# Turning the slot weights (and, in the second slot stage, the normalized tokens) by VectorE and through memory instead of by TensorE, in a three-stage layer on one core

## The chip, the cores and the metric

The kernel runs on one core of one Trainium2 chip. The metric is the device time of one execution in microseconds (us). A core has TensorE (PE in the profile, with its weight loads as PEld), VectorE (DVE), ScalarE (ACT), GpSimd (POOL), SyncE (SP, which here only issues DMAs), and 16 DMA engines between its on-chip memory SBUF and the chip's memory. TensorE's results go to PSUM, from which ACT or DVE copy them to SBUF.

## What is computed

The input x is 16 sequences of 512 tokens with 256 features, in 32-bit floats. The layer is

```
x = x + 0.5 * slot_ffn(layernorm(x))
x = x + attention(layernorm(x))      # causal, rotary, 16 heads of 64
x = x + 0.5 * slot_ffn(layernorm(x)) # the same weights as the first

def slot_ffn(x):
    q = broadcast(slot_query, (16, 16, 256))       # 16 slots for each sequence
    o = q + mha(q, x, x, d_*)                      # "dispatch": the slots gather from 512 tokens, 16 heads of 16
    h = layernorm(o) * ln_g + ln_b                 # slot e has its own expert e
    u, g = silu(h[e] @ W1[e] + b1[e]), silu(h[e] @ Wg[e] + bg[e])
    o = o + (u * g) @ W2[e] + b2[e]                # 16 experts, three weights of 1 MB each
    return mha(x, o, o, c_*)                       # "combine": the tokens read from 16 slots
```

## The kernel before

There are three stages in a row: slot FFN (n = 0), attention, slot FFN (n = 1). x stays in SBUF throughout. TensorE executes its instructions in program order. For ACT, DVE, POOL and SP a scheduler arranges the order in the slot FFN, while the attention is written under `manual_schedule`, in program order.

**Dispatch, the part that is changed.** A loop runs over the 16 sequences ("batches") i, with steps at different distances. The scores of the 256 pairs of slot and head (`FH * NS`, two halves c of 128) against 512 tokens come from one folded matrix `qk`, so each batch needs:

- `normalized` (L216): the layer norm h, with the tokens on the partitions, four DVE instructions. `pair_stats` and `pair_rstd` make mean and 1/std for two batches (PB) at a time.
- `width_first` (L223): hT, with the features on the partitions, by eight TensorE transposes of 128x128 into PSUM, one copy by ACT, one by DVE.
- `slot_weights` (L442): scores p_ds (L449, four matmuls that show as eight records), the row maximum by DVE (L451), its bias by POOL, exp by ACT (L454) into `at`, reciprocals by DVE, scaling by POOL (L458).
- `weights_transposed` (L461): `at` has the slots on the partitions; atT has the tokens there. Eight TensorE transposes p_atT (L467), one copy by ACT (L471), one by DVE (L473).
- `slot_sums` (L476): p_z (L480, 8 matmuls, 16 records), h against atT, copied by DVE into zT (L482).

TensorE's order in an iteration is hT(i), atT(i-2), ds(i-1), z(i-2). After every fourth batch `gathered` (L484) multiplies zT by the value weights (p_mo, 64 records). `half_of_slots` brings half of the slots through output projection (p_o) and layer norm to hE and hET.

**Weights.** `Experts.more` issues one expert weight of 1 MB (48 in all) on SP per call. The first 8 (EARLY) have buffers of their own and are loaded up front; four more (BUFS = 12) lie in pools that take over memory of the dispatch, and the rest follow as buffers come free. Loads 8 and later wait for the last p_mo of the dispatch, whose memory they take. The constants of the stage (`for_slots`, L245: sqbo, dbo, ln_g, ln_b, c_Wk, c_Wv, c_Wq, d_Wo, c_Wo, cbo) and in the first stage the rows of biases are issued on SP ahead of them. `queries(b)` (L366) makes combine's queries p_cq (L369) for batch b; they are spread as fillers through dispatch's end and the experts.

**Attention.** 64 units, a batch with four heads each, in a loop over u = -2 .. 63 in which the steps of units u to u+3 are mixed. For a unit, `exps` makes scores and weights pr, `normalize` scales them on POOL (L864), `Weights.turn` transposes blocks of 32x32 on DVE into sq (L879), `move` (L896) puts the blocks into their places with 16 DMAs of 160 KB on SP, sq to prT, and `sums` (L904, p_av L913) multiplies by the values v (`values`, L805). `leave` (L924) projects the result (p_ay, L929), adds it to x (DVE, L933) and, for a batch's last unit, writes x out (L935). At the end of the loop (u = 62, 63) no new units stand beside these steps.

The functions that the change touches:

Of the kernel before, what the change touches and what calls it, by code (L numbers as in the profile page):

```python
# [15 lines left out]
P = 128  # L16
# [15 lines left out]
EARLY, BUFS = 8, 12  # L32
# [15 lines left out]
def macaron_kernel(ctx: ExitStack, tc: tile.TileContext, a: dict, out: bass.AP):  # L48
# [19 lines left out]
    def by_width(t):  # L68
        return t.rearrange("p (c s) -> p c s", c=NC)

# [80 lines left out]
    def more_constants(su, later):  # L151
# [19 lines left out]
        def pieces():  # L171
# [5 lines left out]
            for k, br in enumerate(brs):  # L177
                for l in range(NL):
                    i = k * NL + l
                    nc.tensor.transpose(pt[:, i * n:(i + 1) * n], br.rearrange("r (p l) -> r l p", l=NL)[:, l],  # L180
                                        ident[:n, :n])
                    nc.vector.tensor_copy(b1g[:, k].rearrange("p e (l q) -> p l e q", l=NL)[:, l],
# [5 lines left out]
    mvs, rstds = {}, {}  # L188
# [18 lines left out]

    def pair_rstd(g, parts=1):
        rstds[g] = small.tile([P, PB * NT], F32, tag=f"rstd{g}", name=f"rstd{g}", bufs=1)
        n = PB * NT // parts  # L210
        for i in range(parts):
            inverse_std(rstds[g][:, i * n:(i + 1) * n], mvs[g][:, i * n:(i + 1) * n, 1], n, f"g{g}_{i}")

    def normalized(pool, b, bufs):

        h = pool.tile([P, NT, D], F32, tag="h", name=f"h{b}", bufs=bufs)  # L216
        for t in range(NT):
            i = (b % PB) * NT + t
            nc.vector.tensor_scalar(h[:, t, :], xs[b][:, t, :], mvs[b // PB][:, i, 0:1],
                                    rstds[b // PB][:, i:i + 1], ALU.subtract, ALU.mult)  # L220
        return h

    def width_first(h, b, hT, c):  # L223

        pt = ps(f"p_hT{b}_{c}")
        for t in range(NT):
            nc.tensor.transpose(pt[:, t * P:(t + 1) * P], h[:, t, c * P:(c + 1) * P], ident)
        if c == 0:
            nc.scalar.copy(hT[:, c, :], pt)
        else:  # L230
            nc.vector.tensor_copy(hT[:, c, :], pt)


    def ffn(n, last, ahead=None):
        with ExitStack() as es:
# [6 lines left out]
            with tc.tile_pool(name=f"early{n}", bufs=1) as ew, tc.tile_pool(name=f"slots{n}", bufs=1) as ss:  # L242
                w = {nm: ss.tile([P, NC, D], F32, tag=nm, name=nm) for nm in ("c_Wk", "c_Wv", "c_Wq")}
# [66 lines left out]
    def slots_and_experts(n, ss, load, w, for_slots, hTs, kT, vT):  # L310
# [52 lines left out]
        def queries(b):  # L363

            pqs = []
            for c in range(NC):  # L366
                pq = ps(f"p_cq{b}_{c}")
                for k in range(NC):
                    nc.tensor.matmul(pq, w["c_Wq"][:, k, c * P:(c + 1) * P], hTs[b][:, k, :],  # L369
                                     start=(k == 0), stop=(k == NC - 1))  # L370
                pqs.append(pq)
            qT = by_width(place(b, f"cq{n}_"))
            for c in range(NC):
                bias = bcol[:, R_CBQ + c:R_CBQ + c + 1]
                if c == 0:
                    nc.scalar.activation(qT[:, c, :], pqs[c], AF.Identity, bias=bias)
                else:
                    nc.vector.tensor_scalar(qT[:, c, :], pqs[c], bias, 1.0, ALU.add, ALU.mult)
            hTs[b] = qT

        with tc.tile_pool(name=f"disp{n}", bufs=2) as dp:
            hs, ats, zT = {}, {}, None
            constants = more_constants(dp, ss) if n == 0 else None
            tail = None
            load.more(EARLY)

            def norm(b):

                if b >= NB:
                    return  # L390
                if b % PB == 0 and (n == 0 or b >= 2 * PB):
                    pair_rstd(b // PB, PB if b == 0 else 1)
                hs[b] = normalized(dp, b, 4)
                if n == 0 and b % PB == 0 and b + PB < NB:
                    pair_stats(b // PB + 1)

            if n == 0:
                pair_stats(0)
            norm(0)
            norm(1)  # L400
            for i in range(NB + 2):
                if i < NB:
                    hTs[i] = by_width(place(i, f"hT{n}_"))
                    for c in range(NC):
                        width_first(hs[i], i, hTs[i], c)
                if i > 2:
                    atT = weights_transposed(dp, i - 2, ats.pop(i - 2))
                if 0 <= i - 1 < NB:
                    ats[i - 1] = slot_weights(dp, i - 1, hTs[i - 1])
                if i == 2:  # L410
                    atT = weights_transposed(dp, 0, ats.pop(0))
                if i == 5 and n == 0:
                    constants()
                if i > 0:
                    norm(i + 1)
                if i >= 2:
                    b = i - 2
                    if b % GB == 0:
                        if b > 0:
# [651 lines left out]
```

## Time and profile before

| | us |
|---|---|
| three timed runs | 2405.11, 2413.08, 2414.31 (median 2413.08) |
| the profiled execution | 2407.17, of which the span of its instructions is 2405.5 |
| dispatch, first stage: first p_ds to end of the last p_mo | 20.80 to 178.92 |
| first stage: experts from the first p_u to the last weights' landing | 191.44 to 288.70 |
| end of the attention's last p_ay | 1998.99 |
| dispatch, second stage: first p_ds to end of the last p_mo | 2006.86 to 2156.70 |
| second stage: the last weights' landing | 2266.21 |

Times in a profile are those of one execution, counted from the start of its span. A line of the timeline or of the chain of waits gives start, length, engine, source line, and how many records ("x8") it takes together; what ended an idle time before it stands behind it in brackets. An fp32 matmul shows as two records. Names such as p_ds or atT are the program's tiles with the numbers left out; L numbers are lines of the kernel before.

### The profile page before, as it was taken

How to read it: one execution, taken by the hardware profiler on the slowest of the kernel's cores; microseconds unless marked ns; L12 is line 12 of the kernel's file. 1: busy time of each engine (PE TensorE's matmuls, PEld its weight loads, DVE VectorE, ACT ScalarE, POOL GpSimd, SP SyncE). 2: the span in 40 equal slices, each digit the busy share in tenths (PEclk: the TensorE clock that was granted, in tenths of full speed). 3: DMA queues.
4: the chain of work that ended last, by engine and by line, in shares of the span. 5: the costliest groups of instructions: out<-in, count | busy, mean ns of one | idle time of the engine just before them, and what ended most of it. 6: DMA issues, size and time to landing. Idle time of an engine off the chain costs nothing.

```text
span 2405.5 us, 42349 instructions
## 1 busy us (share of the span) xinstructions
PE 2331.0 (97%) x14656; PEld 1463.5 (61%) x14656; DVE 1774.9 (74%) x4671; ACT 1069.5 (44%) x2919; POOL 1065.6 (44%) x1692
## 2 busy tenths in 40 slices
PE   7999989899999999999999999999999988999899
PEld 5765478456555555565655555656565555765488
DVE  8542288788888888988888888888888864542287
ACT  4333233355455555554545545545555443323233
POOL 2220044556565655565656555556465531210043
PEclk9999999999999999999999999999999998999999
DMA  9009951254545454545454545455555455019834
GB/s 316 13 2 374 360 126 62 47 120 107 122 107 127 102 132 102 124 108 122 107 131 98 133 105 118 111 118 111 123 107 128 109 130 188 1 44 377 315 110 136
DMA packets 142476, 323.16 MB, mean 134 GB/s; under 512 B 37236, under 2 KB 84408, under 8 KB 134072
## 3 DMA queue, kind: packets, MB, share of 16 engines
q1 hardware_dynamic: 141676, 319.93, 50.1%
q8 instruction: 116, 1.90, 0.3%
q14 instruction: 96, 0.79, 0.1%
q10 hardware_dynamic: 588, 0.54, 0.1%
HBM read 135.84 MB, written 16.78 MB: 63 GB/s over the span
## 4 chain that ended last, share of the span: by engine, by line
PE 83%; DVE 3%; DMA 2%; ACT 2%; SPq 1%; issue 1%; POOL 0%; DVEq 0%; ACTq 0%; POOLq 0%
PE p_as L844 12%; PE p_av L913 12%; PE p_v L805 9%; PE p_k L784 9%; PE p_ay L929 9%; PE p_q L784 9%; PE p_cy L661 4%; PE p_cq L369 4%; PE p_z L480 2%; PE p_ds L449 2%; PE p_cs L630 2%; PE p_u L522 2%; DMA w<-in_e_Wg_dram 1%; ACT pr L856 1%; PE p_catT L651 1%; PE p_y L549 1%
## 5 line engine op out<-in xcount | busy, mean ns | idle before, releaser
L864 POOL TENSOR_SCALAR pr<-pr,ars 128x512 f32<-128x512 f32 (+3 forms) x1024 | 523.6, 532 | 656.0 <-DVE ars L861 656.0
L856 ACT ACTIVATE pr<-pr,amn 128x512 f32<-128x512 f32 (+3 forms) x1024 | 561.6, 550 | 462.2 <-DVE amn L852 462.2
L852 DVE CUSTOM_DVE_ANT_0 pr<-p_as,causal 128x512 f32<-128x512 f32 (+3 forms) x1024 | 434.3, 484 | 98.5 <-PE p_as L844 97.0
L879 DVE STREAM_TRANSPOSE sq<-pr 128x768 f32<-128x768 f32 (+2 forms) x448 | 381.6, 907 | 17.4 <-issue 13.0
L844 PE MATMUL p_as<-k,q 32*128 32x512 f32 (+3 forms) x4096 | 332.1, 449 | 3.6 <-POOL k L795 3.6
L913 PE MATMUL p_av<-prT,v 128*64 128x512 f32 (+3 forms) x2048 | 296.0, 442 | 22.2 <-DMA c_Wk<-in_c_Wk_dram 9.1
L844 PEld LDWEIGHTS p_as<-k,q 32*128 32x128 f32 x4096 | 179.8, 185 | 131.5 <-issue 51.3
L913 PEld LDWEIGHTS p_av<-prT,v 128*64 128x64 f32 x2048 | 142.4, 139 | 182.0 <-issue 152.3
L805 PEld LDWEIGHTS p_v<-wv,ahT 128*128 128x128 f32 x1024 | 189.5, 190 | 98.9 <-issue 46.0
L805 PE MATMUL p_v<-wv,ahT 128*128 128x256 f32 x1024 | 248.9, 386 | 0.0
L929 PE MATMUL p_ay<-wo,aoT 128*128 128x256 f32 x1024 | 238.3, 386 | 0.1
L784 PE MATMUL p_k<-ahT,wk 128*128 128x512 f32 x512 | 236.9, 605 | 0.0
L784 PE MATMUL p_q<-ahT,wq 128*128 128x512 f32 x512 | 230.5, 592 | 0.2 <-ACT ahT L770 0.2
L929 PEld LDWEIGHTS p_ay<-wo,aoT 128*128 128x128 f32 x1024 | 189.3, 190 | 31.3 <-ACT aoT L920 0.6
L856 ACT ACTIVATION_READ_ACCUMULATOR pr<-pr,amn 128x1 f32 x1024 | 191.5, 187 | 0.0
L920 ACT ACTIVATE aoT<-p_av,bcol 128x512 f32<-128x512 f32 x128 | 88.0, 687 | 199.0 <-PE p_av L913 198.9
L784 PEld LDWEIGHTS p_k<-ahT,wk 128*128 128x128 f32 x512 | 92.1, 189 | 126.2 <-issue 115.3
L784 PEld LDWEIGHTS p_q<-ahT,wq 128*128 128x128 f32 x512 | 97.1, 190 | 95.9 <-issue 86.6
L608 POOL TENSOR_TENSOR kbd<-kT,own 128x256 f32<-128x256 f32 x32 | 19.7, 618 | 287.3 <-DVE kT L575 250.6
L661 PE MATMUL p_cy<-vw,catT 128*128 128x256 f32 x512 | 122.1, 382 | 3.0 <-ACT catT L653 3.0
L480 PE MATMUL p_z<-atT,h 128*128 128x256 f32 x512 | 120.2, 389 | 3.6 <-ACT atT L471 3.6
L808 ACT COPY v<-p_v 128x512 f32<-128x512 f32 x128 | 73.4, 573 | 105.3 <-PE p_v L805 105.3
(153 smaller groups left out, 3269.4 us busy)
## 6 DMA issues: line engine op xcount, KB each, us to landing
prT<-sq SPq DMA_DIRECT2D x1024, 160.0 KB
w<-in_e_W_dram SPq DMA_DIRECT2D x64, 1024.0 KB
w<-in_e_Wg_dram SPq DMA_DIRECT2D x32, 1024.0 KB
out_dram<-x SPq DMA_DIRECT2D x64, 256.0 KB
xl<-in_attn_x_dram SPq DMA_DIRECT2D x16, 512.0 KB
xl<-out_dram SPq DMA_DIRECT2D x16, 512.0 KB
x<-in_attn_x_dram SPq DMA_DIRECT2D x15, 512.0 KB
wq<-in_attn_Wq_dram SPq DMA_DIRECT2D x16, 64.0 KB
```

The costliest lines, as they stand in the source:

```text
L369: nc.tensor.matmul(pq, w["c_Wq"][:, k, c * P:(c + 1) * P], hTs[b][:, k, :], start=(k == 0), stop=(k == NC - 1))
L480: nc.tensor.matmul(pz[:, c * 256:(c + 1) * 256], h[:, t, c * P:(c + 1) * P], atT[:, t, :], start=(t == 0), stop=(t == NT - 1))
L661: nc.tensor.matmul(py[:, t * D:(t + 1) * D], atT[:, c, t * P:(t + 1) * P], vws[b][:, c, :], start=(c == 0), stop=(c == NC - 1))
L784: nc.tensor.matmul(pq, self.w[:, k, at:at + P], hTs[self.b][:, k, :], start=(k == 0), stop=(k == NC - 1))
L805: nc.tensor.matmul(pv[:, t * 256:(t + 1) * 256], hTs[b][:, k, (t0 + t) * P:(t0 + t + 1) * P], wv[:, k, hg * HG * DQ:(hg + 1) * HG * DQ], s ...
L844: nc.tensor.matmul(banks[j][:, at:at + w], q[n][j * 32:(j + 1) * 32, i * P:(i + 1) * P], k[n][j * 32:(j + 1) * 32, :w], start=(n == 0), st ...
L852: nc.vector.tensor_tensor_reduce(out=self.at(i, j), in0=banks[j][:, at:at + w], in1=causal[:, S - w:], scale=-1.0 / math.sqrt(DQ), scalar= ...
L856: nc.scalar.activation(self.at(i, j), self.at(i, j), AF.Exp, bias=self.mn[:, i, j:j + 1], scale=-1.0, accum_out=self.rs[:, i, j:j + 1])
L864: nc.gpsimd.tensor_scalar(self.at(i, j), self.at(i, j), self.rs[:, i, j:j + 1], 1.0, ALU.mult, ALU.mult)
L879: nc.vector.transpose(view(self.sq, j * blocks * SQ + dst[0] * SQ, [(blocks * SQ, nh)] + [(s * SQ, n) for s, (_, n) in zip(dst[1:], of)] + ...
L913: nc.tensor.matmul(po[j * DQ:(j + 1) * DQ, :].rearrange("d (a f) -> d a f", a=NSQ)[:, :, t * SQ:], vs[u][:, t, head * DQ:(head + 1) * DQ], ...
L929: nc.tensor.matmul(py[:, t * D:(t + 1) * D], oTs[u][:, pair, (t0 + t) * P:(t0 + t + 1) * P], wo[:, hg * (HG // 2) + pair, :], start=(pair ...
```

## The change

In seven parts; the longer runs of removed lines are left out of the diff, as the functions above show them.

1. **Slot weights.** p_atT, its PSUM tiles and copies go. A new class `Squares` transposes the 32x32 blocks of `at` on DVE (one instruction of 128x512 for each half c, as soon as the half is scaled), writes the result to a scratch tile in memory (`leave`, one DMA of 512 KB on SP) and reads it back with the blocks in their places (`onto`: four DMAs of 32 partitions in the first stage, one in the second, where the layout is `apart`).
2. **Second stage only:** h of batches 2 to 15 takes the same way to hT (one DVE instruction of 128x1024, one write, one read); `width_first` stays for batches 0 and 1, and for all in the first stage.
3. **Engines.** h of batches 2 and later is made by ACT (Identity with scale and shift), not by DVE; the copy of p_z to zT goes from DVE to ACT; the statistics of the first stage are spread over the iterations. DVE, ACT, POOL and SP keep program order in the dispatch loop (`manual_schedule`).
4. **Distances.** TensorE's order becomes hT(i+1), ds(i), z(i-2), and one batch's z comes two iterations after its ds. h has 5 buffers (4), `at` 1 (2), atT 2 (1), sq 2.
5. **Weights.** EARLY is 7 (8), and those loads are issued one in each of the iterations 1 to 7, behind the DMAs of the iteration. c_Wk and c_Wv are loaded after the dispatch, behind the five late weight loads.
6. **Fillers.** queries(0) stands before z(15), queries(1) before the last p_mo, queries(2) to (4) before the experts. hT and the queries' tiles change their layout to blocks of squares. The transposes of the gate's biases (p_b1g) are done together, then their copies.
7. **Last unit of attention.** Unit 63 is not turned by DVE and moved; `turn_at_once` does 40 TensorE transposes into ten PSUM tiles, copied in turn by DVE and ACT, before `sums(62)`; the unit's `values` come before them.

```diff
-EARLY, BUFS = 8, 12
+EARLY, BUFS = 7, 12
...
+    def by_squares(t):
+        return t.rearrange("p (a c n) -> p c a n", a=NSQ, c=NC)
...
+    def pair_shift(g):
+        shifts[g] = small.tile([P, PB * NT], F32, tag="shift", name=f"shift{g}", bufs=2)
+        nc.vector.scalar_tensor_tensor(shifts[g], mvs[g][:, :, 0], -1.0, rstds[g], ALU.mult, ALU.mult)
...
+            rstd = rstds[b // PB][:, i:i + 1]
+            if b < PB:
+                nc.vector.tensor_scalar(h[:, t, :], xs[b][:, t, :], mvs[b // PB][:, i, 0:1], rstd,
+                                        ALU.subtract, ALU.mult)
+            else:
+                nc.scalar.activation(h[:, t, :], xs[b][:, t, :], AF.Identity, bias=shifts[b // PB][:, i:i + 1],
+                                     scale=rstd)
...
+    class Squares:
+        def __init__(self, pool, away, name, src, outer, inner, apart=False):
+            self.name, self.away, self.apart, self.n = name, away, apart, outer * inner * SQ
+            self.sq = pool.tile([P, NSQ, self.n], F32, tag="sq", name=f"sq{name}", bufs=2)
+            self.dst = self.sq.rearrange("p k (i o x) -> p o i k x", i=inner, o=outer)
+            self.src = (src.rearrange("p (o i y k) -> p o i k y", o=outer, i=inner, k=NSQ) if apart else
+                        src.rearrange("p (o i k y) -> p o i k y", o=outer, i=inner, k=NSQ))
+        def turn(self, part=slice(None)):
+            nc.vector.transpose(self.dst[:, part], self.src[:, part])
+        def leave(self):
+            self.mem = self.away.tile([P, NSQ, self.n], F32, tag="away", name=f"away{self.name}")
+            nc.sync.dma_start(self.mem, self.sq)
+        def onto(self, dst):
+            if self.apart:
+                nc.sync.dma_start(dst.rearrange("p (a f) -> p a f", a=NSQ),
+                                  self.mem.rearrange("(a y) k f -> (y k) a f", a=NSQ))
+                return
+            for k in range(NSQ):
+                nc.sync.dma_start(dst[k * SQ:(k + 1) * SQ].rearrange("y (a f) -> y a f", a=NSQ),
+                                  self.mem.rearrange("(a y) k f -> k y a f", a=NSQ)[k])
...
-                w = {nm: ss.tile([P, NC, D], F32, tag=nm, name=nm) for nm in ("c_Wk", "c_Wv", "c_Wq")}
+                w = {nm: ss.tile([P, NC, D], F32, tag=nm, name=nm) for nm in ("c_Wq",)}
...
-        with tc.tile_pool(name=f"disp{n}", bufs=2) as dp:
-            hs, ats, zT = {}, {}, None
+        with tc.tile_pool(name=f"disp{n}", bufs=2) as dp, \
+                tc.tile_pool(name=f"away{n}", bufs=3, space=bass.MemoryType.DRAM) as away:
+            hs, ats, zT, turned, back = {}, {}, None, {}, {}
             constants = more_constants(dp, ss) if n == 0 else None
             tail = None
...
+            direct = NB if n == 0 else PB
+            def width(b):
+                hTs[b] = by_squares(place(b, f"hT{n}_"))
+                for c in range(NC):
+                    width_first(hs[b], b, hTs[b], c)
             if n == 0:
...
+            width(0)
+            if n == 1:
+                pair_rstd(NB // PB - 1)
+            with tc.manual_schedule(engines={mybir.EngineType.DVE, mybir.EngineType.Activation,
+                                             mybir.EngineType.Pool, mybir.EngineType.SP}):
+                for i in range(NB + 2):
+                    stats = [(i + 2 * PB, t) for t in range(NT)] if n == 0 and i + 2 * PB < NB else []
+                    def count(k):
+                        for one in stats[:k]:
+                            token_stats(*one)
+                        del stats[:k]
+                    count(1)
+                    if i + 1 < min(direct, NB):
+                        width(i + 1)
+                    if i + 2 < NB:
+                        hs[i + 2] = normalized(dp, i + 2, 5)
+                    def between():
+                        count(1)
+                        if direct <= i + 2 < NB:
+                            sq = turned[i + 2] = Squares(dp, away, f"h{i + 2}",
+                                                         hs[i + 2].rearrange("p t d -> p (t d)"), NT, NC, True)
+                            sq.turn()
+                            sq.leave()
+                    if i < NB:
+                        at, scaled = slot_weights(dp, i, hTs[i], between)
+                    else:
+                        between()
+                    if i - 1 in back:
+                        atT = dp.tile([P, NT * FH * NS], F32, tag="atT", name=f"atT{i - 1}", bufs=2)
+                        back.pop(i - 1).onto(atT)
+                        ats[i - 1] = atT.rearrange("p (g t c i) -> p t c g i", g=NSQ, t=NT, c=NC)
+                    if i < NB:
+                        scaled(0)
+                        count(2)
+                        scaled(1)
...
+                        sq = back[i] = Squares(dp, away, f"a{i}", at.rearrange("p c s -> p (c s)"), NC, NT, n == 1)
+                        for c in range(NC):
+                            sq.turn(slice(c, c + 1))
+                        if i + 2 in turned:
+                            t = place(i + 2, f"hT{n}_")
+                            hTs[i + 2] = by_squares(t)
+                            turned.pop(i + 2).onto(t)
+                        sq.leave()
...
+                    if 0 < i <= EARLY:
+                        load.more()
+                    if i == 5 and n == 0:
+                        constants()
+                    if i >= 2:
+                        b = i - 2
+                        if b % GB == 0:
+                            if b > 0:
+                                gathered(b // GB - 1, zT, moT, wvm)
+                            zT = dp.tile([P, NC, FH, GB, NS], F32, tag="zT", name=f"zT{b}", bufs=1)
+                        if b == NB - 1:
+                            queries(0)
+                        slot_sums(b, zT, hs.pop(b), ats.pop(b))
+                        if b == NB // 2:
+                            tail = half_of_slots(0)
+                        if b == NB // 2 + 1:
+                            tail()
+                queries(1)
+                gathered(NB // GB - 1, zT, moT, wvm)
+                queries(2)
+                tail = half_of_slots(1)
         gp.close()
         with tc.tile_pool(name=f"late{n}", bufs=1) as lw, \
                 tc.tile_pool(name=f"last{n}", bufs=1, side="right") as rw, \
                 tc.tile_pool(name=f"exp{n}", bufs=2) as ep:
             load.late, load.last = lw, rw
             load.more(BUFS - EARLY)
-            queries(2)
+            for nm in ("c_Wk", "c_Wv"):
+                w[nm] = rw.tile([P, NC, D], F32, tag=nm, name=nm)
+                nc.sync.dma_start(w[nm], a[nm].rearrange("(c p) f -> p c f", p=P))
             queries(3)
+            queries(4)
             tail()
-            experts(ep, load, w, hET, oT, kT, vT, [lambda b=b: queries(b) for b in range(4, NB)])
-
-    def slot_weights(dp, b, hT):
-        at = dp.tile([P, NC, S], F32, tag="at", name=f"at{b}")
+            experts(ep, load, w, hET, oT, kT, vT, [lambda b=b: queries(b) for b in range(5, NB)])
+    def slot_weights(dp, b, hT, between):
+        at = dp.tile([P, NC, S], F32, tag="at", name=f"at{b}", bufs=1)
         rsum = small.tile([P, NC], F32, tag="rsum", name=f"rsum{b}")
         mx = small.tile([P, NC], F32, tag="nmx", name=f"nmx{b}")
         for c in range(NC):
             psc = ps(f"p_ds{b}_{c}")
             for k in range(NC):
-                nc.tensor.matmul(psc, qk[:, k, c * P:(c + 1) * P], hT[:, k, :], start=(k == 0), stop=(k == NC - 1))
+                nc.tensor.matmul(psc.rearrange("p (a n) -> p a n", a=NSQ), qk[:, k, c * P:(c + 1) * P], hT[:, k],
+                                 start=(k == 0), stop=(k == NC - 1))
...
-            nc.scalar.activation(at[:, c, :], psc, AF.Exp, bias=mx[:, c:c + 1], accum_out=rsum[:, c:c + 1])
+            nc.scalar.activation(at[:, c, :].rearrange("p (t a x) -> p t a x", t=NT, a=NSQ),
+                                 psc.rearrange("p (a t x) -> p t a x", t=NT, a=NSQ), AF.Exp,
+                                 bias=mx[:, c:c + 1], accum_out=rsum[:, c:c + 1])
+            if c == 0:
+                between()
         rinv = small.tile([P, NC], F32, tag="rinv", name=f"rinv{b}")
-        nc.vector.reciprocal(rinv, rsum)
-        for c in range(NC):
+        def scaled(c):
+            nc.vector.reciprocal(rinv[:, c:c + 1], rsum[:, c:c + 1])
             nc.gpsimd.tensor_scalar(at[:, c, :], at[:, c, :], rinv[:, c:c + 1], 1.0, ALU.mult, ALU.mult)
...
+        return at, scaled
...
-        nc.vector.tensor_copy(zT[:, :, :, b % GB, :], pz.rearrange("p (c h q) -> p c h q", c=NC, h=FH))
+                nc.tensor.matmul(pz[:, c * 256:(c + 1) * 256].rearrange("p (c g i) -> p c g i", c=NC, g=NSQ),
+                                 h[:, t, c * P:(c + 1) * P], atT[:, t], start=(t == 0), stop=(t == NT - 1))
+        nc.scalar.copy(zT[:, :, :, b % GB, :], pz.rearrange("p (c h q) -> p c h q", c=NC, h=FH))
...
+                pool, tag, bufs = (ap, "v", 1) if u + 1 < nu else (qp, "hT", 2)
+                vs[u] = pool.tile([P, NT, HG * DQ], F32, tag=tag, name=f"v{b}_{hg}", bufs=bufs)
...
+            def turn_at_once(self):
+                prT = prTs[self.u] = ap.tile([P, NSQ, HG, blocks * SQ], F32, tag="sq", name=f"prT{self.nm}")
+                where = {first[t] + i - t: (i, t) for i in range(NT) for t in range(i + 1)}
+                per = S // P
+                for g in range(HG * blocks // per):
+                    pt = ps(f"p_prT{self.nm}_{g}")
+                    for n in range(per):
+                        j, at = divmod(g * per + n, blocks)
+                        i, t = where[at]
+                        nc.tensor.transpose(pt[:, n * P:(n + 1) * P], self.at(i, j)[:, t * P:(t + 1) * P], ident)
+                    dst = prT.rearrange("p a h f -> p a (h f)")[:, :, g * per * SQ:(g + 1) * per * SQ]
+                    dst = dst.rearrange("p a (n x) -> p a n x", n=per)
+                    src = pt.rearrange("p (n a x) -> p a n x", n=per, a=NSQ)
+                    if g % 2:
+                        nc.scalar.copy(dst, src)
+                    else:
+                        nc.vector.tensor_copy(dst, src)
...
+                if old and u + 2 == nu:
+                    values(u + 1, 0)
+                    values(u + 1, 2)
+                    old.turn_at_once()
                 if u >= 0:
                     sums(u, 0)
                     sums(u, 1)
-                if old:
+                if old and u + 2 < nu:
                     old.turn_rest()
                     old.move()
...
-                if 0 <= u + 1 < nu:
+                if 0 <= u + 1 < nu - 1:
                     values(u + 1, 0)
...
+                turns = new and u + 3 < nu
+                if turns:
                     new.turn_most(0)
                     new.turn_most(1)
                 if u >= 0:
                     leave(u, 2)
-                if new:
+                if turns:
                     new.turn_most(2)
                     new.turn_most(3)
                     new.turn_corner()
```

## The prediction

> **What bounds the kernel now.** I read the totals by engine first, then the slices of the span, then the chain that ended last, and then TensorE's timeline where the slices dip. From the page:
>
> ```profile
> PE 2331.0 (97%) x14656; PEld 1463.5 (61%) x14656; DVE 1774.9 (74%) x4671; ACT 1069.5 (44%) x2919; POOL 1065.6 (44%) x1692
> PE   7999989899999999999999999999999988999899
> DMA  9009951254545454545454545455555455019834
> GB/s 316 13 2 374 360 126 62 47 120 107 122 107 127 102 132 102 124 108 122 107 131 98 133 105 118 111 118 111 123 107 128 109 130 188 1 44 377 315 110 136
> ```
>
> TensorE is the bound almost everywhere. In slices 2, 3 and 35 (the slot stages) the DMA engines are nearly idle; in slices 4, 5, 37 and 38 they are the second bound (the experts' weight stream). So work taken from TensorE in a slot stage counts only if the stream behind it may start earlier. The chain in the second slot stage, start, length, link:
>
> ```profile
> 2029.91 0.87 PE p_hT L227 x8
> 2030.79 0.87 PE p_atT L467 x8
> 2031.66 3.44 PE p_ds L449 x8
> 2035.10 3.45 PE p_z L480 x16
> ...
> 2249.11 17.06 DMA w<-in_e_Wg_dram
> ```
>
> A batch is four links with no gap: 8.63 us. The last line is the expert stage's end waiting for its last weights, so that end follows the start of the stream. TensorE's timeline around the last attention units:
>
> ```profile
> 1965.78 6.07 PE L913 MATMUL p_av<-prT,v 128*64 128x512 f32 x32 [5.65 <-DMA prT<-sq]
> 1971.78 3.72 PE L805 MATMUL p_v<-wv,ahT 128*128 128x256 f32 x16
> 1975.34 3.62 PE L929 MATMUL p_ay<-wo,aoT 128*128 128x256 f32 x16
> 1988.05 6.87 PE L913 MATMUL p_av<-prT,v 128*64 128x512 f32 x32 [9.10 <-DMA c_Wk<-in_c_Wk_dram]
> 1994.85 4.14 PE L929 MATMUL p_ay<-wo,aoT 128*128 128x256 f32 x16
> ```
>
> Two waits for the transposed weights of units 62 and 63, 5.65 and 9.10 us; the c_Wk named is a neighbour on SP of the prT moves. After them the sums take 6.07 and 6.87 us against 4.46 in the steady state. Last, windows (length, busy time with counts for PE, PEld, DVE, ACT, POOL, then granted clock, DMA share, GB/s):
>
> ```profile
> 6.00:22.00 16.00, 11.26 (x42) 9.04 (x43) 11.53 (x48) 3.70 (x7) 1.18 (x4) 1.00 1.08 380
> 1600.00:1700.00 100.00, 100.00 (x627) 59.15 (x626) 84.30 (x229) 49.68 (x153) 58.42 (x89) 1.00 0.54 119
> 1966.00:1988.00 22.00, 12.95 (x64) 8.56 (x62) 8.61 (x14) 2.54 (x4) 0.12 (x1) 0.81 0.67 151
> 2020.00:2130.00 110.00, 110.00 (x689) 80.07 (x689) 60.86 (x138) 35.58 (x75) 25.70 (x73) 1.00 0.08 31
> ```
>
> The first is x read from memory in rows of 1 KB, the second steady attention, where nearly all traffic is prT<-sq inside SBUF: 119 at share 0.54, so 220 GB/s at full. The fourth is the second slot stage: TensorE never idle, DMA at 8%.
>
> **Base.** The profiled execution took 2407.17 us, its span 2405.5, so 1.7 lies outside. The three timed runs have median 2413.08; the mean of the four is 2409.9. Savings are worked out in the span and taken from 2409.9. About 0.5% (12 us) is what a measurement can tell from no change.
>
> **Price of a trip through memory.** No row shows SBUF to memory and back. The nearest: x's loads, 380 GB/s; the output's last 256 KB write, issued at 2402.25 and over at 2405.5, 3.25 us of which 0.7 is data, so about 1.0 before and 1.6 behind the data. For 512 KB at 380 GB/s data take 1.4: 3.9 us a way, 7.8 both. The other end is prT's 220 GB/s: 2.4 of data, 9.8 both. I take 380, since both ways have memory at one end and rows of 1 KB or more, as the x loads have; 220 stays for the range.
> The Trainium skill (DMA: Bandwidth & Descriptors, Anatomy of one DMA) puts about 2.0 us plus bytes/436 GB/s on a DMA: 3.2 us a way; it would shorten each exposed trip below by about 1.4 us and lower the sum by some 4. The same skill (VectorE: DVE Perf Modes, Rules for kernel authors) advises TensorE for a 128x128 transpose where PSUM may be the target, because VectorE only does 32x32 blocks: it speaks against this change where the trip is exposed; no run here shows such a trip.
>
> **First stage.** Removed: 16 x 0.87 = 13.9 us of p_atT on TensorE, with its two copies (0.59 ACT, 0.68 DVE). New period 0.87 + 3.44 + 3.45 = 7.76. The regrouped bias transposes (61 us) give perhaps 3 back. But a(0)'s write stands on SP behind all constants, which SP issues until 39.65 in before, 38.2 without c_Wk and c_Wv. It lands at 42.1, its four reads at about 46, and z(0), at 33.12 before, starts at 46.2; TensorE has run out of work at 34, so it idles 12 us once and restarts at a low clock (z 5.4 rather than 3.45, as before after a 2.27 idle). From 46.2 to the end of ds(15): 13 z, 13 hT, 13 ds, 3 p_mo of 1.03, 1.9 for the clock, 2 for biases = 107.6, so 153.8. a(15) needs 4.2 (reduce 0.69, bias 0.4, exp 0.88, reciprocal, scale 0.69, turn 0.67, hand-overs) and its trip 7.8: z(15) at 166; z(13), z(14) and cq(0) cover all but 2 of that. z(15), cq(1), p_mo end at 174.1, against 178.92: 4.8 earlier. In the expert stage the stream carries 5 late loads and c_Wk, c_Wv (2.69 us per MB, 14.8) ahead of w12 where 4 loads and a 2.8 us gap stood (13.6): 1.2 back. **Gain 3.6**; with no early stall 15, with a trip of 9.8 about 0.
>
> Layer norm goes from DVE (4 x 0.405) to ACT (4 x 0.515), zT's copy too: ACT then has per batch 2 x 0.88 + 0.59 + 0.6 + 2.06 = 5.0, DVE about 4 and 5 with the second stage's 1.2 us turn, POOL 2.2. All lie under 6.89, so I cost them at nothing; uncovered, ACT's would be 0.44 a batch. Matmuls read the turned tiles in runs of 32 elements; av reads prT so already and 128x512 takes 0.442 there, not more than p_as with 0.449: nothing.
>
> **Last unit.** ay(61) ends at 1960.1. v(63) (3.7) fills part of the 5.65 idle; POOL ends unit 63's normalization at 1965.2, and 40 transposes (0.109 each, 4.4) follow, done at 1968.2; their ten copies of 0.6 to 0.7 on two engines (3.3) lie beside av(62). Then av(62) 4.46, 0.9 of hand-over, ay(62) 3.45, av(63) 4.46, 0.9, ay(63) 3.5: 1985.9 against 1998.99. **Gain 13.1**; if the clock stays low as after the present waits, 9. SP drops 16 of its 32 last moves, so what queues behind them is earlier.
>
> **Second stage.** Entry as before, so ds(0) at 2006.86 - 13.1, about 1994. TensorE keeps 6.89 a batch from batch 2 on, 8.63 - 6.89 = 1.74 less, 28 us if nothing else comes last. Something does. Each iteration sends h out, a back, h back, a out, and in iterations 1 to 7 a 1 MB load, all on SP in order. h's read waits until its write has landed; behind that read stand a's write, the load and the next h's write. The loop is 1.0 (start) + 1.4 (h in) + 1.4 (a out) + 2.7 (load) + 1.4 (next h out) + 1.6 (landing; a's read lies inside) = 9.5 us; without the load 6.8, just under TensorE. h(2) is turned behind ds(0)'s first reduce, by 1998.3, and its trip of 7.8 holds ds(2) to 2006; TensorE is through with ds(1) at 1994 + 5.1 + 3.5 = 2002.6, so 3.5 idle. ds(10) then starts at 2006 + 6 x 9.5 + 2 x 6.89 + 2 x 1.03 = 2078.8, about 1 later with a slower clock (2095.43 before); ds(15) ends at 2119.5; a(15)'s 4.2 + 7.8 sets z(15) at 2131.5 to 2132; cq(1) and p_mo end at 2140.2 against 2156.70. Gain so far 16.5, of which 13.1 is the last unit's; the later stream costs 1.2 again: **15.3 for both**.
>
> **Sum.** 2409.9 - 3.6 - 15.3 = 2391.
>
> **Rivals.**
> Hidden trip (0.16): the load overlaps the landing waits and TensorE sets 6.89 throughout; ds(10) 20 us earlier: 2371. For it: DMA at 8% in this stage now, and 3.15 MB per iteration is 8.2 us at 380. Against it: 8.2 is already over 6.89.
> Shared rate (0.20): out and in at once reach about 300 GB/s; 1.75 us per 512 KB makes the loop 10.7 and 8.0, so 6 x 1.2 + 7 x 1.1 = 15 more: 2406, no difference to be told. The saving is there on TensorE's list and comes back as idle time.
> Slow trip, slower than before (0.16): memory trips move as prT's, at 205 to 240 GB/s. 2.2 us per 512 KB gives loops of 11.9 and 9.2: 6 x 2.4 + 7 x 2.3 = 31 more, 2422; at 2.56 us 57 more, 2448; middle 2435. It decides from some 235 GB/s down, where the second stage's loop passes 8.63 even without a load. For it: 220 is what this queue reaches in most of the trace; against it: the 380 of each memory row.
> That the change does not do what it says would show as p_atT still on TensorE; the instruction lists leave no room for it.
>
> **How the numbers follow.** Forecast 0.48 (2380 to 2402), the rivals as given. Faster by over 0.5% (below 2401): most of the forecast and the hidden trip, 0.60; within 0.5%: its upper edge and the shared rate, 0.24; slower: 0.16. The range is 2368 to 2422: it takes in the hidden trip and the shared rate and leaves out most of the slow trip.
>
> **What would show it.** Right: z(0) at about 46 with an idle of 12 ended by DMA atT; p_z and p_ds alone on the chain from batch 2 of the second stage, with idle of 2 to 3 us ended by DMA hT in iterations 2 to 7 and none after; ay(63) ending near 1982 in the new span (1985.9 less the first stage's 3.6); the last weights 3 to 4 us earlier in the first stage. Wrong: hT waits past iteration 8 (slow trip), none at all (hidden trip), waits on ACT's h or copies (an engine I cost at nothing), or an expert stage whose end does not move with p_mo.

## The result and the profile after

The changed kernel takes 2404.74 us (median of 15 runs, 2401.6 to 2408.1) against 2410.47 for the kernel before in the same sessions: ratio 0.9976, 95% interval 0.9968 to 0.9985. It is faster by 5.7 us, where 2391 (19 us faster) was forecast. The time lies in the stated range, but the gain is a third of what was expected, and by the text's own bound of 0.5% it counts as no difference.

First the totals, the slices of TensorE's clock and of the DMA engines (page, parts 1 and 2):

```profile
PE 2303.1 (96%) x14328; PEld 1432.7 (60%) x14328; DVE 1774.8 (74%) x4603; ACT 1120.2 (47%) x3024; POOL 1064.6 (44%) x1692
PE   6999899899999999999999999999999997899899
PEclk9999999999999999999999999999999998899999
DMA  8739852254545454555554545545455546859834
GB/s 270 220 127 399 331 126 62 48 120 106 121 109 124 105 129 105 121 113 117 113 126 104 125 109 117 117 109 121 114 116 118 116 93 239 297 187 399 326 111 136
```

TensorE is busy 28 us less, and the span is only 5.6 us shorter: the rest came back as idle time. The new dips are in the first slice and in slices 34 and 35 (1980 to 2100 us), the start of either dispatch, and in the latter two the granted clock is lower as well. In slices 35 and 36 the DMA engines, nearly idle before (1 and 44 GB/s), now move 297 and 187.

TensorE's timeline (start, length, what, idle before it and what ended it), first around the first stage's early wait, then in the second stage:

```profile
45.55 5.16 PE L576 MATMUL p_z<-atT,h 128*128 128x256 f32 x16 [12.15 <-DMA atT<-awaya]
...
172.12 1.10 PE L590 MATMUL p_mo<-zT,wvm 128*32 128x64 f32 x64
...
1980.42 3.29 PE L1044 MATMUL p_ay<-wo,aoT 128*128 128x256 f32 x14 [0.16 <-ACT aoT L1035]
...
2004.13 5.37 PE L552 MATMUL p_ds<-hT,qk 128*128 128x512 f32 x8 [4.06 <-DMA hT<-awayh]
...
2020.28 5.38 PE L576 MATMUL p_z<-atT,h 128*128 128x256 f32 x16 [3.73 <-DMA atT<-awaya]
...
2040.03 6.31 PE L576 MATMUL p_z<-atT,h 128*128 128x256 f32 x16 [3.74 <-DMA atT<-awaya]
...
2059.24 3.69 PE L576 MATMUL p_z<-atT,h 128*128 128x256 f32 x16 [1.35 <-DMA atT<-awaya]
...
2070.01 6.67 PE L576 MATMUL p_z<-atT,h 128*128 128x256 f32 x16 [3.65 <-DMA atT<-awaya]
...
2095.14 1.13 PE L373 MATMUL p_o<-d_Wo,moT 128*128 128x256 f32 x4 [2.82 <-DVE moT L595]
2096.11 5.29 PE L552 MATMUL p_ds<-hT,qk 128*128 128x512 f32 x8
...
2151.11 1.10 PE L590 MATMUL p_mo<-zT,wvm 128*32 128x64 f32 x64
```

The first stage is as forecast: 12 us of idle once, z(0) at 45.55, p_mo done at 173.2 (178.9 before). The last unit too: p_ay ends at 1983.7 (1999.0). But the second dispatch ends at 2152.2 (2156.7): it entered 14.9 us early and leaves 4.5 early. Its loop waits for atT again and again, and each idle of 3.65 us or more is followed by a group that takes 5.2 to 6.7 us instead of 3.6 or 3.7; behind an idle of 1.35 us the z has its full speed, 3.69. The Trainium skill (TensorE: Matmul & The Clock Gate, What's actually happening) has the clock fall to half after an idle window of some 3.4 us. The lines with 3.65 us and more agree; but the ds shortly behind the idle of 2.82 us took 5.29 too, so an idle shorter than the skill's figure can be followed by a slow group.

What stands behind the waits, from the chain that ended last (start, length, link):

```profile
2057.82 2.00 DVE sqh L265
2059.82 0.03 DVE nmx L555
2059.84 8.55 DMA awayh<-sqh
...
2068.52 1.99 DVE sqh L265
2070.50 0.03 DVE nmx L555
2070.53 8.28 DMA awayh<-sqh
```

In these two iterations h's write needs 8.3 to 8.6 us to land, behind a read, a's write and a load in the queue; only then may DVE turn the next h, since there are two buffers (sq) for all turned blocks. And that turn takes 2.0 us, not the 1.2 that the forecast took. The windows (length, busy PE, PEld, DVE, ACT, POOL with counts, granted clock, DMA share, GB/s) of the loaded iterations and of the first stage's experts:

```profile
2010.00:2070.00 60.00, 47.47 (x207) 30.27 (x206) 35.22 (x48) 25.66 (x57) 12.68 (x36) 0.91 0.89 312
190.00:280.00 90.00, 85.27 (x790) 43.66 (x788) 22.96 (x63) 27.21 (x53) 0.00 (x0) 1.00 1.02 404
```

In the loop the engines are 89% busy and move 312 GB/s: 351 GB/s at a share of 1. The weight stream alone reaches 404 at 1.02.

### The profile page after: what moved, and what is told of

Its sections match the earlier page's. It is cut to its first block, busy times and chain, and to the rows that moved or that the text cites. A ratio compares the mean times of both kernels' runs of the same rounds, so it can differ in the third digit from the quotient of the medians.

```text
span 2399.9 us, 41890 instructions
## 1 busy us (share of the span) xinstructions
PE 2303.1 (96%) x14328; PEld 1432.7 (60%) x14328; DVE 1774.8 (74%) x4603; ACT 1120.2 (47%) x3024; POOL 1064.6 (44%) x1692
## 4 chain that ended last, share of the span: by engine, by line
PE 85%; DVE 5%; DMA 5%; ACT 2%; issue 1%; SPq 1%; POOL 0%; DVEq 0%; ACTq 0%; POOLq 0%
PE p_as L940 12%; PE p_av L1028 11%; PE p_v L901 9%; PE p_k L879 9%; PE p_ay L1044 9%; PE p_q L879 8%; PE p_cy L757 4%; PE p_cq L416 4%; PE p_z L576 4%; PE p_ds L552 3%; PE p_cs L726 2%; PE p_u L618 2%; DMA w<-in_e_Wg_dram 1%; ACT pr L952 1%; DMA awaya<-sqa 1%; PE p_catT L747 1%
## 5 line engine op out<-in xcount | busy, mean ns | idle before, releaser
L975 DVE STREAM_TRANSPOSE sq<-pr 128x768 f32<-128x768 f32 x441 | 375.6, 906 | 13.1 <-issue 13.0
L576 PE MATMUL p_z<-atT,h 128*128 128x256 f32 x512 | 125.9, 403 | 29.4 <-DMA atT<-awaya 29.2
L576 PEld LDWEIGHTS p_z<-atT,h 128*128 128x128 f32 x512 | 101.9, 202 | 58.8 <-issue 40.0
```

What stands on the lines that cost most here:

```text
L576: nc.tensor.matmul(pz[:, c * 256:(c + 1) * 256].rearrange("p (c g i) -> p c g i", c=NC, g=NSQ), h[:, t, c * P:(c + 1) * P], atT[:, t], sta ...
L975: nc.vector.transpose(view(self.sq, j * blocks * SQ + dst[0] * SQ, [(blocks * SQ, nh)] + [(s * SQ, n) for s, (_, n) in zip(dst[1:], of)] + ...
```

## The experiments

Each was timed against the kernel before in the same session (2410 to 2411). Below, "2-9" is the time from the second stage's ds(2) to its ds(9), which holds the loads, and "dispatch" is from its first p_ds to the end of its last p_mo, from each run's profile. These two come from one execution each: the two profiles of h_by_pe differ by 2.7 us in the dispatch.

| kernel | 2-9 | dispatch | median | ratio to before, 95% |
|---|---|---|---|---|
| before | 61.7 | 149.8 | 2410.47 | |
| changed | 72.4 | 160.2 | 2404.74 | 0.9968 to 0.9985 |
| tail_only | 61.7 | 150.6 | 2396.54 | 0.9922 to 0.9952 |
| h_by_pe | 58.0 | 139.2 | 2382.26 | 0.9862 to 0.9891 |
| h_by_pe_again | 59.6 | 141.9 | 2382.96 | 0.9874 to 0.9903 |
| load_in_gap | 75.9 | 165.3 | 2404.08 | 0.9963 to 0.9984 |
| not_apart | 91.6 | 184.0 | 2425.85 | 1.0039 to 1.0078 |
| four_sq | 70.3 | 157.3 | 2397.11 | 0.9935 to 0.9965 |
| loads_after | 55.1 | 142.8 | 2387.71 | 0.9896 to 0.9925 |
| a_first | 69.2 | 155.3 | 2398.00 | 0.9922 to 0.9962 |
| a_first_four_sq | 69.1 | 155.1 | 2396.67 | 0.9927 to 0.9957 |
| first_by_pe | 67.8 | 150.8 | 2394.54 | 0.9925 to 0.9960 |
| late_h | 67.3 | 154.8 | 2392.65 | 0.9916 to 0.9952 |
| const_late | 58.0 | 139.3 | 2377.87 | 0.9859 to 0.9893 |

**The last unit alone.** The diff is that of part 7 on the kernel before.

> The kernel before with part 7 alone (unit 63 turned by TensorE). Theory: the last unit is worth what the two traces show around it, some 13.9 us, whatever the slot stages do: about 2396, with the second dispatch as long as before (149.8 us from its first p_ds to the end of its last p_mo). Rival: the gain needs the new entry into the second stage too, or is taken back in the second stage's DMA-bound experts; then 2405 or more, like the changed kernel.

14.8 us faster (its interval reaches from 11.6 to 18.8): the whole of this term, and more than twice what the full change brings. All else in the change together loses 9 us.

**h by TensorE, the weights through memory.**

```diff
-            direct = NB if n == 0 else PB
+            direct = NB
```

> The changed kernel, but in the second stage too h is transposed by TensorE; only the slot weights go through memory. Theory that the second stage is held by its memory trips: the traffic of an iteration falls from 3.15 to 2.1 MB, TensorE sets 7.76 a batch as in the first stage, and the second dispatch takes about 141 us from its first p_ds to the end of its last p_mo (first stage 152.4 less the early idle of 12) against 160.3: some 19 us faster than the changed kernel at that point, about 2387 in all. Rival, that the lost time lies in the order on DVE, ACT and SP rather than in traffic: the dispatch stays near 155 to 160 and the time near 2400.

The first theory holds, with a little more than expected (141 and 2387): 29 us faster than before, 22 faster than the changed kernel, by one line. TensorE's timeline shows the loop as planned, hT, ds and z back to back:

```profile
2015.62 3.60 PE L552 MATMUL p_ds<-hT,qk 128*128 128x512 f32 x8
2019.05 3.62 PE L576 MATMUL p_z<-atT,h 128*128 128x256 f32 x16
2022.51 1.04 PE L243 MATMUL p_hT<-ident,h 128*128 128x128 f32 x8
2023.38 3.60 PE L552 MATMUL p_ds<-hT,qk 128*128 128x512 f32 x8
```

Over the dispatch its windows read, and those of the changed kernel for comparison below:

```profile
1989.00:2128.00 139.00, 136.14 (x778) 91.71 (x776) 74.83 (x137) 73.72 (x156) 33.87 (x96) 1.00 0.50 175
```

```profile
1992.00:2152.00 160.00, 137.44 (x665) 86.17 (x664) 91.42 (x137) 67.13 (x142) 33.81 (x96) 0.92 0.71 244
```

The changed kernel has 112 transposes fewer and is busy *longer*, 137.4 against 136.1, since its clock is 0.92 rather than 1.00. What h's trip took from TensorE (12 us) the lower clock alone took back; the idle time comes on top.

**What holds the loop: three edits of order and buffers.** In load_in_gap, `load.more()` stands between the turn of a and the read of h; in four_sq there is

```diff
-EARLY, BUFS = 7, 12
+EARLY, BUFS = 6, 12
-            self.sq = pool.tile([P, NSQ, self.n], F32, tag="sq", name=f"sq{name}", bufs=2)
+            self.sq = pool.tile([P, NSQ, self.n], F32, tag="sq", name=f"sq{name}", bufs=4)
```

and in a_first `sq.leave()` stands ahead of `turned.pop(i + 2).onto(t)`.

> The changed kernel with the second stage's 1 MB load moved on SP: from behind a's write to ahead of h's read, so that its data fill the wait for h's write to land. Bytes and number of DMAs are the same. If the bytes set the loop (3.15 MB at the 320 GB/s that the trace shows), ds(2) to ds(10) stays at 80 us and the total at 2405. If the chain of landing waits sets it, the DMA share rises from 0.89 towards 1.05, the loaded iterations fall to about 8.4, ds(2) to ds(10) to about 70, and the total to about 2396.

> The changed kernel with four buffers of turned blocks (sq) instead of two; to make room EARLY is 6 instead of 7, so a sixth late weight load follows each dispatch (2.7 us a stage on the experts' stream). Theory of the buffer: with two, h's turn waits until the last h's write has landed behind a read, a write and a load (8.3 to 8.6 us on the chain, with 2.0 of turn: the 10 us of an iteration); with four that wait goes, the bytes at 380 GB/s (8.2 us) come next, and ds(2) to ds(10) falls from 80 to 66 to 70 us, the total to 2395 to 2400 with the later streams. Theory of the bytes at 320 GB/s, or of the landing waits of one trip: it stays at 78 to 80, the total at 2405 to 2410.

> The changed kernel with a's write issued ahead of h's read instead of behind it, in the second stage: while SP waits for h's write to land, a's write already runs. What is open: of the loop of 10 us, 3.15 MB at 351 GB/s (312 at a DMA share of 0.89) take 9.0; is the other 1.0 SP's waiting in order? If so ds(2) to ds(9) falls from 72.4 to about 66 and the DMA share rises above 0.95; the total to about 2399. If the idle engines are due to the two buffers or to the transfers themselves, no change: 72 and 2405.

> a_first with four buffers of turned blocks and EARLY 6, so that neither SP's order nor the buffers hold a write back. If order and buffers each cover for the other (one wait takes the other's place), this one reaches what the bytes allow: 9.0 an iteration, ds(2) to ds(9) at 64 to 66, and a total some 5 below four_sq (2397), 2392. If the transfers alone set the loop, ds(2) to ds(9) stays at 70 as in four_sq and the total at 2397.

load_in_gap: wrong, ds(2) to ds(10) grew from 79.8 to 84.6 and the DMA share fell to 0.84; the load now stands ahead of a's write and read, and TensorE waits for both kinds of trip. four_sq: h's wait for its buffer was on the chain, yet taking it away leaves ds(2) to ds(10) at 78.6, because the next wait (landing, behind the same queue) takes its place. The two runs with four buffers also carry six loads in the loop instead of seven, as EARLY is 6, so the 2 us that four_sq gains in 2-9 need not come from the buffers. a_first, with two buffers and seven loads, fills the queue:

```profile
2010.00:2070.00 60.00, 48.38 (x215) 30.24 (x214) 36.91 (x51) 26.38 (x59) 13.63 (x41) 0.96 0.98 329
```

The share rises from 0.89 to 0.98, and the rate only to 329 GB/s; 2-9 falls by 3.2 to 69.2, half of what was expected, and with four buffers as well, and one load fewer, it is 69.1. So order was worth 3 us of the loop. (The totals of four_sq and a_first fall by some 7 us, of which the dispatch shows 3 and 5; the rest stays open.) What is left is transfer: at 329 GB/s, 3.15 MB take 9.6 us (2-9 of a_first is 9.9 an iteration), and TensorE's 6.89 can't be reached while an iteration carries a load and both trips. The next run tests it by taking the loads away.

**The loads out of the loop.**

```diff
-                    if 0 < i <= EARLY:
+                    if n == 0 and 0 < i <= EARLY:
                         load.more()
...
+                if n == 1:
+                    load.more(EARLY)
                 queries(1)
                 gathered(NB // GB - 1, zT, moT, wvm)
```

> The changed kernel with the second stage's seven early loads issued behind the dispatch loop instead of one in each of its iterations 1 to 7. Theory of the buffer: the write of h then has only a read and a write ahead of it, lands in about 5 us, and the iteration is 2.0 + 5 = 7 us, close to TensorE's 6.89: ds(2) to ds(10) near 58 to 60 against 80; the experts' stream is later by some 4 us against p_mo; total near 2390. Theory that the strided turns and the order on the engines hold it without the loads too: ds(2) to ds(10) at 70 or more and the total at 2400 or more.

2-9 falls by 17 to 55.1, ds(2) to ds(10) to 63.5 (58 to 60 expected, 70 or more by the rival), and the total by 17 to 2387.71: seven loads cost the loop 17 us. Behind the dispatch they cost a few: from the last p_mo to the end of the span the profile has 251.5 us against 247.7 in the changed kernel (the expectation had some 4). From 2010 to 2070 us the DMA engines are now 79% busy and move 272 GB/s, and the chain has no DMA in it for long stretches, but DVE, ACT and POOL in turn:

```profile
2023.88 2.04 DVE sqh L265
2025.91 0.57 DVE nmx L557
2027.06 0.79 ACT at L560 x2
2027.95 1.02 DVE sqa L265
2029.03 1.05 DVE sqa L265
```

Turns of 2.0 and twice 1.0 us, in DVE's fixed order, are the next limit, at 7.9 us an iteration (2-9 over seven). So even without loads h's trip does not bring the dispatch (142.8) under that of h_by_pe (139.2 and 141.9).

**The turns with contiguous reads.** `apart` is False everywhere.

> The changed kernel with the second stage's turns as in the first: DVE reads blocks of contiguous rows, and each read back is four DMAs of 128 KB instead of one of 512 KB. If the strided turns (2.0 us for h, 1.04 for half of a, against 1.2 and 0.69) are a part of the loop, h leaves 0.8 us and a 0.7 us earlier, and ds(2) to ds(10) falls from 80 to about 75, the total to about 2400. If the bytes set it, no change (2405). The six more issues of some 0.44 us on SP cost 2.6 an iteration; if SP's issues are on the chain, slower, 2410 or more.

The turn falls as priced, but the four reads cost far more (groups on DVE from 1995 to 2125 us, count, busy, mean ns, idle before, of the changed kernel and then of not_apart, which has come to its twelfth turn by then):

```profile
L265 DVE STREAM_TRANSPOSE sqh<-h 128x1024 f32<-128x1024 f32 x14 | 28.2, 2017 | 11.1 <-DMA awayh<-sqh 6.9 <-ACT h L235 4.2
```

```profile
L265 DVE STREAM_TRANSPOSE sqh<-h 128x1024 f32<-128x1024 f32 x12 | 14.9, 1242 | 31.4 <-DMA awayh<-sqh 30.5 <-ACT h L235 0.8
```

1.24 us a turn instead of 2.02, and 21 us slower in all: the last case of the expectation. Each read takes 1.73 us of SP or more, and the traffic fell to 229 GB/s in the same 60 us (2010 to 2070).

**The early wait and the trips without loads.** first_by_pe turns a(0) and a(1) of both stages by TensorE, ahead of z(0) and z(1), as the kernel before does; late_h also has `direct = 10` in the second stage. Both have EARLY 6, so one more load comes after each dispatch.

> h_by_pe of the runs before (2382) with the weights of batches 0 and 1 of both stages turned by TensorE as in the kernel before; `at` has two buffers, EARLY is 6. The first stage's 12 us of idle ahead of z(0) should fall to 1 to 3, since a(0) is scaled at 33.8; the second stage's 2.2 goes too. That is 11 to 12 us less at each p_mo's end, less 2.7 a stage for the sixth late load: about 2376. If the idle is bound by something else (statistics on DVE, x's arrival), z(0) stays past 40 and the time at 2382 or more.

> first_by_pe, but in the second stage h of batches 10 to 15 goes through memory, so that its trips fall in iterations 8 to 13, which carry no load. If a trip is harmless where the queue has room, six times 0.87 = 5 us less than first_by_pe. If the strided turns and landing waits hold these iterations as well (2.0 + 5 = 7.0 us and a first trip that is exposed), no gain or a loss of a few us.

first_by_pe missed: 12 us slower than h_by_pe. z(0) starts at 39.25 instead of 45.1, then z(1) waits again, and by z(1) the lead is gone (54.95 against 55.43); in the second stage each of the two waits for copies that stand in ACT's and DVE's fixed order, and the dispatch is 11.6 longer.

```profile
39.25 2.08 PE L599 MATMUL p_z<-atT,h 128*128 128x256 f32 x4 [4.47 <-ACT atT L590]
...
54.95 5.41 PE L599 MATMUL p_z<-atT,h 128*128 128x256 f32 x16 [3.34 <-ACT atT L590]
```

late_h against it: a dispatch longer by 4.0, totals whose intervals overlap. So h's trip shows no gain even where no load runs beside it.

**SP ahead of the first write.** On h_by_pe:

```diff
-            constants = more_constants(dp, ss) if n == 0 else None
+            constants = None
...
-                    if i == 5 and n == 0:
+                    if i == 2 and n == 0:
+                        constants = more_constants(dp, ss)
+                    if i == 6 and n == 0:
                         constants()
```

> h_by_pe, with the first stage's bias rows (eleven DMAs, 8 us of SP) issued in iteration 2 instead of ahead of the loop, and their transposes one iteration later. In h_by_pe a(0) is turned at 29.4 and its write is issued at 37.6, when SP is through with them. Theory that the idle ahead of z(0) is SP's: the write leaves at about 30, z(0) starts near 37 instead of 45, both p_mo ends and the total are about 8 us earlier: 2374. Rival: eleven issues in iteration 2 hold the next read back by as much (z(2) or z(3) then waits), and the total stays at 2380 to 2382.

> h_by_pe a second time, beside the next run, so that the two can be compared directly: 2382 again.

2377.87 against 2382.96 for h_by_pe beside it; the intervals overlap. SP issues a(0)'s write at 30.66 rather than 37.6, but its read only at 36.69: the write lands after 6.0 us (2.9 in the changed kernel), and x and constants are in the queue ahead of it. z(0) starts at 41.2, the later reads are held up by 0.6 and 1.4, and p_mo ends 0.5 to 1.6 earlier. It is the fastest kernel here, 32 us (1.2%) faster than before; how much of that is this edit's stays open.

## Why the prediction was wrong

**The first stage** was right: idle 12 (12.15), z(0) at 46.2 (45.55), p_mo's end 4.8 earlier (5.7), gain 3.6. The profile of before had 1.00 as its clock from 300 to 320 us and that of the changed kernel 0.83; tail_only, whose program is the kernel before's up to the last unit, had 0.85 there, and so had every other run's (0.77 to 0.85), so the difference is that one execution's and not the change's. tail_only and the changed kernel share the last unit: their last p_ay ends at 1988.9 and 1983.7, so the first stage is worth 5.2.

**The last unit** was right: 13.1 forecast, 14.8 in tail_only.

**The second stage is the step that failed.** The forecast from ds(0) to the end of p_mo was 146.2; it took 160.2. Entry, first trip and ds(2) were right (12.0 forecast, 12.2). ds(2) to ds(10) took 79.8 instead of 73.8, ds(10) to the end of ds(15) 46.8 instead of 39.7, the rest 21.5 instead of 20.7: 14 us, which is the miss of the total. The loop of the memory trips can be read on SP's list, as the distance between one read of h and the next (here of h(2), h(3), h(10) and h(11), and the last load):

```profile
2000.30 0.38 SPq L273 DMA_DIRECT2D hT<-awayh  x1
...
2007.05 0.37 SPq L273 DMA_DIRECT2D hT<-awayh  x1
...
2069.75 0.43 SPq L345 DMA_DIRECT2D w<-in_e_W_dram  x1
2070.53 0.94 SPq L269 DMA_DIRECT2D awayh<-sqh  x1
...
2078.86 0.37 SPq L273 DMA_DIRECT2D hT<-awayh  x1
...
2085.71 0.37 SPq L273 DMA_DIRECT2D hT<-awayh  x1
```

- **The loaded loop was mis-sized.** The loops without a load right ahead of the loaded ones and behind them took 6.75 and 6.85 us, as forecast (6.8). The seven with a load, from h(3) to h(10), took 71.8 us, 10.26 each instead of 9.5. The price of the trips' data was taken from x's loads, 380 GB/s. A trip alone is as quick as that or quicker (a(0)'s write landed in 2.85 us where 3.9 was forecast), but 3.15 MB in 10.26 us are 307 GB/s, and with the better order of a_first writes and reads that share the queue with loads moved 329 with the engines at 0.98. In the sum, the DMA's data were added up only along the chain of landings, and the bytes of an iteration (8.2 us at 380) were checked once, in a rival, and not set as a floor: at 329 the floor is 9.6, above the forecast loop of 9.5.
- **One loaded loop was left out.** The load of an iteration stands ahead of the next iteration's write of h, so the load of iteration 7 delays h(10): seven loaded loops lie ahead of ds(10), and the sum had six and two without. By the forecast's own prices that is 2.6 us; the price of the loop makes 5.3; the two p_mo (2.1) that the sum put on top of the loops hardly added to them.
- **The turns were not free.** Turns of 128x1024 took 2.0 us instead of 1.2, and of 128x512 1.1 instead of 0.67: they were priced by rows with contiguous reads (128x768 takes 0.91 in the profile before), and `apart` reads with a stride of four elements. They hold DVE's fixed order, in which the results of p_mo wait: p_o's idle of 2.82 and the slow ds behind it are most of the 7 us after ds(10). No load is needed for that: loads_after has 45.5 us from ds(10) to the end of ds(15). With contiguous reads, in not_apart, p_o follows z with no idle and it is 43.4. "All lie under 6.89, so I cost them at nothing" failed here.

The rival that came true is the shared rate (0.20): "out and in at once reach about 300 GB/s", 2406. Its sign, "The saving is there on TensorE's list and comes back as idle time", is what the profile shows, though the waits are for atT where the forecast had named hT: a's read stands behind h's write and the load too. The forecast preferred 380 because each memory row has it; but each of those rows moves data one way only. That its total came so near is in part luck: it made the loops without a load longer as well, 8.0 us, where the two beside the loaded ones took 6.75 and 6.85; half of the miss lies behind ds(10), in what the turns hold up. Nor do all the rivals' figures follow from their own terms: 1.75 us a trip gives loops of 10.55 and 7.85 and a total of 2404; 2.56 us gives 45 more, 2436; and the loop without a load passes 8.63 from about 260 GB/s down, not 235. The forecast itself does not use them.

The rule of the Trainium skill that speaks against the change (VectorE: DVE Perf Modes, Rules for kernel authors: TensorE for 128x128 where PSUM may be the target) is borne out for h (22 us) and not for the weights: in h_by_pe they go through memory, and with parts 3 to 6 of the change both dispatches are faster than the kernel before's (152.1 against 158.1, and 139.2 against 149.8). The Trainium skill (DMA: Bandwidth & Descriptors, Anatomy of one DMA) fits 2.0 us plus bytes/436 GB/s to DMAs that GpSimd issues, from which an estimate for 512 KB is 3.2 us; these here are issued by SP, and alone 2.85 and 2.7 were measured, on the loop's chain 5.1 to 8.6.

Open: whether more buffers bring anything by themselves, and whether h's trip would pay with contiguous turns and one DMA at once; no layout with both was tried.

## What to carry to other kernels

Before work is moved from a busy engine to the DMA queue, add up all bytes that the queue carries in one iteration, at a rate measured with reads and writes mixed, and set the sum beside the busy engine's period; latency chains come after that. Two savings of the same kind need not go together: the first fitted under the period, the second pushed the queue over it and lost more than the first had brought. Count which loop each load delays: one that is issued behind an iteration's own DMAs is paid by the next. Measure parts alone before they are judged together: here the last unit brought 14.8 us, the slot weights with parts 3 to 6 about 14, and h's trip lost 22.

## What the runs showed of the hardware

- The DMA engines moved 404 GB/s at a share of 1.02 with loads alone, and 329 at 0.98 with half-megabyte writes and reads among the loads (a_first).
- A DVE transposition of 32x32 blocks took 1.24 us for 128x1024 with contiguous reads and 2.02 with a stride of 16 bytes (0.69 and 1.09 for 128x512).
- One read as four DMAs of 32 partitions instead of one of 128: 1.73 us of SP or more against 0.37, and 229 GB/s against 312.
- A write issued beside nothing landed in 2.9 us, the same write with loads still in the queue in 6.0.
